# Local attention blocks: norms made per chunk, an early exponential, and ones ahead of the first block

## The chip, the cores and the metric

The kernel runs on one core of one Trainium2 chip. The metric is the device time of one execution in microseconds (us); of several runs the median is given. The engines are named as in the profile: PE is the matrix engine (PEld its weight loads), DVE the vector engine, ACT the scalar engine, POOL the GpSimd engine, and SP issues most of the transfers.

## The reference

The reference is a decoder of twelve sublayers over x of shape 16 x 64 x 128 (1024 tokens of 128 features), each followed by a residual addition and a layer norm. The change touches the third sublayer alone, a stack of two local attention layers over 16 sequences of 64 tokens. One such layer computes:

```
h = shift_token(x)                     # half of the features come from the token before
q, k, v = split(h @ wqkv)              # 8 heads of 64
q = l2norm(q) * q_scale;  k = l2norm(k) * k_scale
q, k = rotary_xpos(q, k)               # q*cos*scale + rotate_half(q)*sin*scale
o = softmax(8 * q k^T, causal in windows of 64) v
x = x + o @ wo
x = x + (a * gelu(g)) @ w2 + b2        # a, g from layernorm(shift_token(x)) @ w1 + b1
```

Here `l2norm(t)` is `t / max(norm(t), 1e-12)`. The other sublayers are attention with and without a context, a linear recurrence, and routed feed-forward layers.

## The kernel before, in words

The 1024 tokens are handled as two halves of 512. Each half is a Python generator (`first_stream`) that hands back control after every small stage, and `side_by_side` takes turns between the two halves, with half 0 five stages ahead. So the instructions of half 1's local block stand between those of half 0's local block, or of its neighbours. The program is written with a framework that schedules the instructions when it is compiled: each engine gets one fixed list, in an order that the framework chooses from what depends on what and from when buffers become free. At run time every engine goes through its list in order; an instruction that waits holds up all that stand behind it on that engine. A small change in the source can therefore change the lists around it.

The local block is `local_half(h)`. It runs two layers, and for each it works on four chunks of 128 tokens, two pairs `u` = 0 and 1 of two chunks each. The stages of a layer:

- `rotate(u)` makes, for both chunks of a pair, queries and keys on PE (L151, into a PSUM tile `qk` from a pool of two), squares them on ACT (L827), sums the squares per head on DVE (L830), multiplies by cosine tables (L834, one DVE instruction on 128 x 1024) and by sine tables with the two half-heads exchanged (L848, two DVE instructions on 128 x 512), and adds the two products on POOL (L854). The squares of both chunks are collected in one tile `ss` of 128 x 32. After the second chunk's cosine product the sums are clamped from below on DVE (L844) and rooted on ACT (L845); at the end of the stage DVE takes the reciprocal (L856). ACT holds the tables of only some functions at a time, so a root after an exponential is preceded by a table load, and so is the exponential after that.
- `values(u)` makes the values on PE and copies them from PSUM on ACT (L868).
- `flip(u)` multiplies both chunks by the reciprocals on POOL (L878), transposes them on PE (L884) and copies the result from PSUM on ACT (L885).
- `weights(u)` makes the scores on PE (L896 and a mask, L905), their maximum (L917) and the difference (L918) on DVE, and the exponential on ACT (L921). `turn(u)` transposes the weights (L930, copies L931).
- `weigh(u)` multiplies by the values (L948), divides by the sums (L958, L959 on DVE); `gather` transposes the outcome (L973, copies L974), and `put(u)` applies `wo` (L151) and adds the input (L988 on DVE).
- Then comes the feed-forward part: a shift of half the features (L151 into `psh`, copy L1020), statistics (L1026, L1028), an inverse deviation in eleven small DVE steps (L176 to L183), the normalization on DVE (L1031), six products of ones and four transposes on PE (L1040), an activation (L1044), two POOL additions for the residual (L1049, in the second layer also L1053), and the two products with the gelu between them (L1061, L1064; the PSUM tiles are `pg` and `pa`).

The ones are products of a constant matrix of ones in bf16 that `keep_busy` (L156) writes into a PSUM tile which the real work overwrites. Ahead of the first local block, cross attention (`xa`) ends with a layer norm whose output is transposed (L244) and copied to `hs` in two steps (L246, L247) between which ACT makes an exponential of the other half (L556). POOL also fills memory for a later sublayer with memsets (L417, L419) beside the last block.

Of the kernel before, what the change touches and what calls it, by code (L numbers as in the profile page):

```python
# [11 lines left out]
F32 = mybir.dt.float32  # L12
# [3 lines left out]
AF = mybir.ActivationFunctionType  # L16
ALU = mybir.AluOpType
AX = mybir.AxisListType
# [3 lines left out]
P = 128  # L22
# [15 lines left out]
class Kernel:  # L38
# [761 lines left out]
    def local_half(self, h):  # L800

        nc = self.nc
        work, psc, pt = self.aw, self.psc, self.pt
# [3 lines left out]
        for l in range(2):  # L807
            tag = f"lb{l}{h}"
# [3 lines left out]
            turned, qkT, es, eTs, oTs, aos = {}, {}, {}, {}, {}, {}  # L812

            def rotate(u):


                both = []
                ss = work.tile([P, 2, 16], F32, tag="ss", name=f"{tag}_ss{u}")
                for r in range(2):
                    c = u * 2 + r  # L820
                    qk = psc.tile([P, 2, HALF], F32, tag="sc", name=f"{tag}_qk{c}")
                    for t in range(2):
                        self.group(
                            qk[:, t, :], [(hs[:, bass.ts(c, P)], wqk[:, bass.ts(t, HALF)])]
                        )
                    t2 = self.buf(4, [2, 8, 64], f"{tag}_t2{c}")
                    nc.scalar.activation(  # L827
                        t2.rearrange("p t n d -> p (t n d)"), qk.rearrange("p t m -> p (t m)"), AF.Square
                    )
                    nc.vector.tensor_reduce(  # L830
                        ss[:, r, :], t2.rearrange("p t n d -> p (t n) d"), AX.X, ALU.add
                    )
                    t1 = self.buf(4, [2, HALF], f"{tag}_t1{c}")
                    nc.vector.tensor_tensor(  # L834
                        t1.rearrange("p t (n d) -> p t n d", d=64),
                        qk.rearrange("p t (n d) -> p t n d", d=64),
                        cos.unsqueeze(2).to_broadcast([P, 2, 8, 64]),
                        ALU.mult,
                    )
                    if r == 1:  # L840

                        root = work.tile([P, 64], F32, tag="root", name=f"{tag}_rs{u}")[:, 0:32]
                        flat = ss.rearrange("p r n -> p (r n)")
                        nc.vector.tensor_scalar(flat, flat, 1e-24, None, ALU.max)  # L844
                        nc.scalar.activation(flat, flat, AF.Sqrt)  # L845
                    for side in range(2):
                        to, of = slice(32 * side, 32 * side + 32), slice(32 - 32 * side, 64 - 32 * side)
                        nc.vector.tensor_tensor(  # L848
                            t2[:, :, :, to],
                            qk.rearrange("p t (n d) -> p t n d", d=64)[:, :, :, of],  # L850
                            sin[:, :, to].unsqueeze(2).to_broadcast([P, 2, 8, 32]),
                            ALU.mult,
                        )
                    nc.gpsimd.tensor_tensor(t1, t1, t2.rearrange("p t n d -> p t (n d)"), ALU.add)  # L854
                    both.append(t1)
                nc.vector.reciprocal(root, flat)  # L856
                turned[u] = (both, root)

            def values(u):
                for b in range(u * 4, u * 4 + 4, 2):  # L860
# [11 lines left out]
            def flip(u):  # L872

                to = self.buf(8, [8, 256], f"{tag}_qkT{u}")
                both, rs = turned.pop(u)
                for r, t1 in enumerate(both):
                    t3 = t1.rearrange("p t (n d) -> p (t n) d", d=64)
                    nc.gpsimd.tensor_tensor(  # L878
                        t3, t3, rs[:, bass.ts(r, 16)].unsqueeze(2).to_broadcast([P, 16, 64]), ALU.mult
                    )  # L880
                    for t in range(2):
                        ps = pt.tile([P, 4, P], F32, tag="t", name=f"{tag}_pf{u}{r}{t}")
                        for c in range(4):
                            nc.tensor.transpose(ps[:, c, :], t1[:, t, bass.ts(c, P)], ident)  # L884
                        nc.scalar.copy(to[:, 4 * t : 4 * t + 4, bass.ts(r, P)], ps)  # L885
                qkT[u] = to
# [92 lines left out]
            def put(u):  # L979
# [13 lines left out]
                )  # L993

            rotate(0)
            values(0)
            yield
            rotate(1)
            flip(0)
            yield  # L1000
            weights(0)
            values(1)
            yield
            turn(0)
            flip(1)
            yield
            weigh(0)
# [69 lines left out]
            if l == 0:  # L1077
                x_in = self.buf(2, [4, D], f"{tag}_x2")
                nc.vector.tensor_tensor(x_in, ps, base, ALU.add)
                self.shifted(self.psum(pt, f"{tag}_px"), h, x_in)  # L1080
                yield
            else:
                y = self.new_y("lb", h)
                nc.vector.tensor_tensor(y, ps, base, ALU.add)
                flip = self.close(pt, h, y, "lb", ones=2 + 5 * h)
                yield "last"
                flip()
# [960 lines left out]
```

## Time and profile before

| | |
|---|---|
| median of 3 runs | 878.72 us (876.24 to 880.52) |
| the profiled execution's own time | 877.26 us |
| its span, first to last instruction | 875.1 us |
| mean granted PE clock | 0.892 of full |
| PE, DVE, ACT, POOL busy | 738.4, 482.1, 354.9, 255.2 us |
| stretch of the four local blocks | from 113 to 312 us of the span |
| the add L854 | 16 times, 2354 ns |
| the scaling L878 | 16 times, 1902 ns |
| the clamp L844 | 8 times, 171 to 1490 ns |
| the reciprocal L856 | 8 times, 335 to 344 ns |
| the root L845 | 8 times, 229 to 230 ns, with 5 table loads of 1283 ns |

How to read it: a row of the chain of waits gives a start, a duration and the engine and line that the end of the program was waiting for at that time. A row of the timeline gives the start, the busy time, the engine, the line and the operation, with tiles and shapes, and in brackets how long the engine had been idle and which work released it. A row of the windows gives the stretch, its length, the busy time of PE, PEld, DVE, ACT and POOL with instruction counts, the granted clock of PE as a share of the full clock, the share of the transfer engines, and GB/s. One row can stand for several like instructions ("x2").

### The profile page before, as it was taken

Reading aid. Unit: us, or ns where it says so; the run is one execution under the profiler, and the core shown is the slowest. Engines: PE = TensorE matmul, PEld = TensorE weight load, DVE = VectorE, ACT = ScalarE, POOL = GpSimd, SP = SyncE. Lnnn points to the kernel's source line nnn. Section 1 sums busy time; section 2 is a strip of 40 time slices with the busy share of each in tenths; the row PEclk is TensorE's granted clock in tenths of the full one; section 3 lists DMA queues with packets and bytes.
Section 4 is the critical chain, followed back from the end, with each engine's and each line's share of the span. In section 5 each row is a group of like instructions: output and inputs, shape, how many; then the busy total and the mean of one; then the engine's idle time right before and its main releaser. Section 6 shows DMA issues by size and latency. Waiting matters only on the chain.

```text
span 875.1 us, 17527 instructions
## 1 busy us (share of the span) xinstructions
PE 738.4 (84%) x7115; PEld 467.3 (53%) x7117; DVE 482.1 (55%) x1103; ACT 354.9 (41%) x584; POOL 255.2 (29%) x289
## 2 busy tenths in 40 slices
PE   7888989779787899889998899958858999967991
PEld 2334547456464666457473567624534665744671
DVE  5556466674856647365446565552451856654564
ACT  1223457355454534464632454421205544511230
POOL 2324133260615412223035300035052011016632
PEclk8899989989999898999996899977967899956996
DMA  7900000000000000410000000051206632021102
GB/s 277 270 14 13 1 1 2 13 1 2 1 1 1 1 1 1 152 42 1 1 1 1 1 3 1 1 164 42 57 25 192 194 119 76 14 108 43 40 28 85
DMA packets 34504, 43.65 MB, mean 50 GB/s; under 512 B 7524, under 2 KB 26469, under 8 KB 33784
## 3 DMA queue, kind: packets, MB, share of 16 engines
q1 hardware_dynamic: 32344, 38.26, 14.1%
q0 software_dynamic: 2080, 4.26, 1.7%
q8 instruction: 58, 0.95, 0.4%
q14 instruction: 22, 0.18, 0.1%
HBM read 34.31 MB, written 11.61 MB: 52 GB/s over the span
## 4 chain that ended last, share of the span: by engine, by line
PE 52%; DVE 16%; POOL 7%; issue 6%; ACT 5%; DMA 3%; another core or an unknown queue 1%; SPq 1%; POOLq 0%; DVEq 0%; ACTq 0%
PE xa_sc L494 4%; PE xa_av L588 4%; PE xa_pt L567 3%; PE at_sc L494 2%; PE sw_pe L151 2%; PE lb_pf L884 2%; PE at_pt L567 2%; PE at_av L588 2%; POOL lb_t L878 2%; PE xa_sc L505 1%; PE lb_po L151 1%; DVE xa_e L553 1%; DVE lb_t L848 1%; PE xa_pt L156 1%; DVE lb_t L834 1%
## 5 line engine op out<-in xcount | busy, mean ns | idle before, releaser
L552 DVE TENSOR_REDUCE xa_mx<-xa_sc 128x16 f32<-128x1024 f32 x40 | 48.8, 1219 | 65.8 <-PE xa_sc L505 43.4
L854 POOL TENSOR_TENSOR lb_t<-lb_t,lb_t 128x1024 f32<-128x1024 f32 x16 | 37.7, 2354 | 98.9 <-DVE lb_t L848 94.7
L570 ACT COPY xa_eT<-xa_pt 128x512 f32<-128x512 f32 x80 | 45.0, 586 | 42.5 <-PE xa_pt L567 41.7
L156 PEld LDWEIGHTS <-ones_b 128*128 128x128 bf16 x327 | 32.2, 106 | 55.0 <-issue 36.4
L556 ACT ACTIVATE xa_e<-xa_e 128x1024 f32<-128x1024 f32 x40 | 42.3, 1058 | 44.1 <-DVE xa_e L553 44.0
L494 PE MATMUL xa_sc<-xa_km,xa_q 32*64 32x256 f32 x640 | 54.8, 407 | 1.5 <-DVE xa_e L553 0.9
L455 POOL TENSOR_SCALAR xa_km<-xa_k,const 128x512 f32<-128x512 f32 x40 | 27.3, 699 | 96.5 <-ACT xa_k L443 57.6
L567 PE MATMUL xa_pt<-const,xa_e 128*128 128x128 f32 x320 | 48.7, 279 | 2.1 <-ACT xa_e L556 2.1
L553 DVE TENSOR_TENSOR xa_e<-xa_sc,xa_mx 128x1024 f32<-128x1024 f32 x40 | 48.7, 1218 | 2.5 <-DVE xa_mx L552 0.5
L567 PEld LDWEIGHTS xa_pt<-const,xa_e 128*128 128x128 f32 x320 | 39.9, 144 | 14.6 <-ACT xa_e L556 4.6
L588 PEld LDWEIGHTS xa_av<-v,xa_eT 128*64 128x64 f32 x1280 | 40.6, 138 | 8.7 <-issue 6.5
L588 PE MATMUL xa_av<-v,xa_eT 128*64 128x18 f32 (+1 forms) x1280 | 44.4, 209 | 0.0
L151 PE MATMUL lb_qk<-w,lb_hs 128*128 128x512 f32 x64 | 34.1, 656 | 8.6 <-DVE lb_t L848 4.8
L494 PEld LDWEIGHTS xa_sc<-xa_km,xa_q 32*64 32x64 f32 x640 | 24.6, 137 | 21.6 <-issue 16.2
L830 DVE TENSOR_REDUCE lb_ss<-lb_t 128x16 f32<-128x1024 f32 x16 | 19.5, 1218 | 25.9 <-ACT lb_t L827 25.9
L205 POOL TENSOR_TENSOR rstd_xa<-mv_xa,eps 128x4 f32<-128x4 f32 x8 | 1.6, 201 | 109.7 <-DVE mv_xa L201 109.7
L156 PE MATMUL xa_pt<-ones_b 128*128 128x512 bf16 x80 | 30.3, 392 | 1.4 <-DVE xa_ao L601 1.4
L884 PE MATMUL lb_pf<-const,lb_t 128*128 128x128 f32 x128 | 22.3, 337 | 10.3 <-POOL lb_t L878 10.2
L878 POOL TENSOR_TENSOR lb_t<-lb_t,lb_rs 128x1024 f32<-128x1024 f32 x16 | 30.1, 1902 | 0.0
L151 PE MATMUL tt_ph<-tt_w,tt_xs 128*128 x40 | 23.8, 679 | 2.9 <-remote 2.9
L884 PEld LDWEIGHTS lb_pf<-const,lb_t 128*128 128x128 f32 x128 | 19.4, 177 | 12.7 <-POOL lb_t L878 11.7
L1356 POOL DMA_INDIRECT tt_got<-tt_in,tt_ids x20 | 19.6, 978 | 18.8 <-DVE tt_ids L1333 6.6
(479 smaller groups left out, 1734.0 us busy)
## 6 DMA issues: line engine op xcount, KB each, us to landing
sw_gu<-in_sw_gu SPq DMA_DIRECT2D x4, 1024.0 KB, 9.0
at_mem<-at_rsb SPq DMA_DIRECT2D x16, 256.0 KB, 2.8
at_rel<-at_mem SPq DMA_DIRECT2D x32, 128.0 KB, 3.0
w<-in_w SPq DMA_DIRECT2D x1, 3114.0 KB, 12.6
sw_dn<-in_sw_dn SPq DMA_DIRECT2D x4, 512.0 KB, 7.3
tt_w<-in_tt_w SPq DMA_DIRECT2D x2, 1024.0 KB, 8.7
tt_b<-in_tt_b SPq DMA_DIRECT2D x1, 2048.0 KB, 7.4
sw_in<-in_zeros SPq DMA_DIRECT2D x1, 1472.0 KB, 11.5
```

The source lines that it names most:

```text
L151: self.nc.tensor.matmul(out, lhsT, rhs, start=n == 0, stop=n == len(pairs) - 1)
L156: self.nc.tensor.matmul(out, self.ones_b, self.ones_b.unsqueeze(1).to_broadcast([P, 4, P]), start=True, stop=True)
L494: nc.tensor.matmul(sc[64 * j : 64 * j + 64, gg, at : at + 256], q[r, t], part[r, :, t] if local else part[r, :, :], start=not masked or (p ...
L552: nc.vector.tensor_reduce(mx, scored, AX.X, ALU.max)
L553: nc.vector.tensor_tensor(e3, scored, mx.unsqueeze(2).to_broadcast([P, 16, S]), ALU.subtract)
L556: nc.scalar.activation(e3, e3, AF.Exp, scale=scale)
L567: nc.tensor.transpose(ps[:, bass.ts(n, P)], blocks[:, bass.ts(n, P)], self.g("ident"))
L570: nc.scalar.copy(eT[:, gg, :], ps)
L588: nc.tensor.matmul(av[64 * j : 64 * j + 64, pr, hp, :, :], eT[:, gg, at : at + 64], v[:, b, hp, :, :], start=True, stop=True,)
L854: nc.gpsimd.tensor_tensor(t1, t1, t2.rearrange("p t n d -> p t (n d)"), ALU.add)
L878: nc.gpsimd.tensor_tensor(t3, t3, rs[:, bass.ts(r, 16)].unsqueeze(2).to_broadcast([P, 16, 64]), ALU.mult)
L884: nc.tensor.transpose(ps[:, c, :], t1[:, t, bass.ts(c, P)], ident)
```

## The change

The tile of sums is made per chunk (128 x 16, two buffers). Right after a chunk's sums are made they are clamped and rooted in place; the reciprocal is taken in place behind the sine products; and the scaling on POOL moves from `flip` to `rotate`, directly behind the chunk's add. At the end of the second pair a small exponential of 8 columns with scale 0 is made into a tile `ready` that nobody reads. In front of the very first product of the first block, six products of ones are written into its PSUM tile. The arithmetic of the outcome is unchanged.

```diff
-                ss = work.tile([P, 2, 16], F32, tag="ss", name=f"{tag}_ss{u}")
                 for r in range(2):
                     c = u * 2 + r
                     qk = psc.tile([P, 2, HALF], F32, tag="sc", name=f"{tag}_qk{c}")
+                    if (tag, c) == ("lb00", 0):
+                        for _ in range(6):
+                            self.keep_busy(qk[:, 0, :])
...
+                    ss = work.tile([P, 16], F32, tag="ss", name=f"{tag}_ss{c}")
                     nc.vector.tensor_reduce(
-                        ss[:, r, :], t2.rearrange("p t n d -> p (t n) d"), AX.X, ALU.add
-                    )
+                        ss, t2.rearrange("p t n d -> p (t n) d"), AX.X, ALU.add
+                    )
+                    nc.vector.tensor_scalar(ss, ss, 1e-24, None, ALU.max)
+                    nc.scalar.activation(ss, ss, AF.Sqrt)
...
-                    if r == 1:
-
-                        root = work.tile([P, 64], F32, tag="root", name=f"{tag}_rs{u}")[:, 0:32]
-                        flat = ss.rearrange("p r n -> p (r n)")
-                        nc.vector.tensor_scalar(flat, flat, 1e-24, None, ALU.max)
-                        nc.scalar.activation(flat, flat, AF.Sqrt)
...
+                    nc.vector.reciprocal(ss, ss)
                     nc.gpsimd.tensor_tensor(t1, t1, t2.rearrange("p t n d -> p t (n d)"), ALU.add)
+                    t3 = t1.rearrange("p t (n d) -> p (t n) d", d=64)
+                    nc.gpsimd.tensor_tensor(
+                        t3, t3, ss.unsqueeze(2).to_broadcast([P, 16, 64]), ALU.mult
+                    )
                     both.append(t1)
-                nc.vector.reciprocal(root, flat)
-                turned[u] = (both, root)
+                if u == 1:
+
+                    ready = work.tile([P, 8], F32, tag="ready", name=f"{tag}_ready", bufs=1)
+                    nc.scalar.activation(ready, ss[:, 0:8], AF.Exp, scale=0.0)
+                turned[u] = both
...
-                both, rs = turned.pop(u)
-                for r, t1 in enumerate(both):
-                    t3 = t1.rearrange("p t (n d) -> p (t n) d", d=64)
-                    nc.gpsimd.tensor_tensor(
-                        t3, t3, rs[:, bass.ts(r, 16)].unsqueeze(2).to_broadcast([P, 16, 64]), ALU.mult
-                    )
+                for r, t1 in enumerate(turned.pop(u)):
```

## The prediction

> **What bounds the kernel now.** I read the page's busy line and chain shares, then the chain in order of time over the local blocks, then the timeline of one block, then one-microsecond windows around the first block.
>
> ```profile
> PE 738.4 (84%) x7115; PEld 467.3 (53%) x7117; DVE 482.1 (55%) x1103; ACT 354.9 (41%) x584; POOL 255.2 (29%) x289
> ...
> PE 52%; DVE 16%; POOL 7%; issue 6%; ACT 5%; DMA 3%; another core or an unknown queue 1%; SPq 1%; POOLq 0%; DVEq 0%; ACTq 0%
> ```
>
> PE is the busiest, but only half of the chain is PE. The change touches four blocks, with their first products at 113, 163, 214 and 265 us; I call them A (layer 0, half 0), B (layer 0, half 1), C (layer 1, half 0) and D (layer 1, half 1). In the chain, C looks like this (B the same, shifted):
>
> ```profile
> 139.26 1.28 ACT L556
> ...
> 223.51 1.19 DVE lb_t L848 x2
> 224.85 0.71 POOL lb_t L854
> 225.56 1.59 issue
> 227.16 3.77 POOL lb_t L878 x2
> 230.97 0.67 PE lb_pf L884 x4
> ```
>
> Inside a block the end is set by DVE (a chunk costs 1.13 + 1.13 + 1.20 us: square sum, cosine product, two sine products), then POOL's add of the second chunk and, behind it, both scalings (3.77), then PE's flip. The first row is a table load on the path in A. The same block in the timeline:
>
> ```profile
> 221.12 2.36 POOL L854 TENSOR_TENSOR lb_t<-lb_t,lb_t 128x1024 f32<-128x1024 f32 x1 [27.92 <-DVE lb_t L848]
> ...
> 223.12 0.39 DVE L844 TENSOR_SCALAR lb_ss<-lb_ss 128x32 f32<-128x32 f32 x1
> 223.43 1.27 DVE L848 TENSOR_TENSOR lb_t<-lb_qk,lb_sin 128x512 f32<-128x512 f32 x2
> ...
> 235.48 0.17 DVE L844 TENSOR_SCALAR lb_ss<-lb_ss 128x32 f32<-128x32 f32 x1
> 235.56 1.28 DVE L848 TENSOR_TENSOR lb_t<-lb_qk,lb_sin 128x512 f32<-128x512 f32 x2
> ...
> 240.66 1.28 ACT L921 ACT_TABLE_LOAD   x1
> ...
> 241.96 1.06 ACT L921 ACTIVATE lb_e<-lb_e 128x1024 f32<-128x1024 f32 x1
> ...
> 242.94 2.20 DVE L1031 TENSOR_SCALAR lb_hn<-lb_y,lb_mv,lb_rstd 128x128 f32<-128x128 f32 x4
> 243.01 1.27 POOL L1049 TENSOR_TENSOR lb_base<-lb_y,wide 128x512 f32<-128x512 f32 x1
> ```
>
> The clamp of the norms (L844) takes 0.17 when POOL rests and 0.39 when it meets POOL's add: 223.12 + 0.39 = 223.51, the add ends at 223.48, and the next DVE instruction starts only then. So this DVE form is held until POOL's instruction ends. L1031 is held in the same way by L1049 (2.20 for four; free, they cost 0.34 each). The exponential starts 0.02 after its table load, though its input was ready at 240.83. The first block:
>
> ```profile
> 110.00:111.00 1.00, 0.62 (x3) 0.28 (x2) 1.00 (x2) 0.34 (x1) 0.00 (x0) 1.00 0.03 8
> 111.00:112.00 1.00, 0.00 (x0) 0.00 (x0) 0.37 (x1) 0.83 (x2) 0.00 (x0) 1.00 0.00 0
> 112.00:113.00 1.00, 0.00 (x0) 0.00 (x0) 0.00 (x0) 0.99 (x2) 0.00 (x0) 0.54 0.00 0
> 113.00:114.00 1.00, 0.90 (x1) 0.50 (x2) 0.00 (x0) 0.04 (x1) 0.00 (x0) 0.50 0.00 0
> ```
>
> Third figure from the right is the granted clock: it falls to 0.50 at 112.1 and returns at 118.9, just over A's first products. Their first chunk takes 3.80 us on the chain, in B 2.00.
>
> **The ones (A).** Six more 128x512 bf16 products, 0.25 each (six before the flips of L1040: 1.47). Compiled, four stand in front of the four transposes L244, the rest between them; their PSUM buffer has been free since 105.9. PE idles there (0.5 busy a microsecond), so they cost nothing to 0.15 us. PE's busy share from 108.7 to 112.1 rises from about 0.32 to 0.65; stretches of that length at 0.53 and above kept the clock (221.3 to 224.7: 0.53), one at 0.47 lost it. The first square moves from 116.91 to 115.25. If they fail, it stays.
>
> **Norms by chunk.** Per block: four clamps, roots and reciprocals of 16 columns in place of two of 32. On DVE +2 clamps (0.17 long, but the next instruction starts 0.08 later, as at 235.48) and four reciprocals for two (0.34 now for 32 columns, 0.17 for 4 columns as in L958, so about 0.24 for 16; 0.17 to the next start for 0.26): 0.32 us in all. ACT: +2 roots of at most 0.23, and the root with its table load (1.28) now stands in front of the second value copy L868, which comes 1.3 later; the weighing that reads it is a stage away, so it costs nothing, and 1.3 a block if it were not. POOL does the same 8 instructions a block, but now add, scale, add, scale: the first scaling no longer waits behind the second add. The compiled order of the changed kernel shows what this moves: the odd chunk's clamp now stands right behind its square sum, where POOL's first add is running. Behind it wait the cosine and sine products, for which PE's next product and the other half's reciprocals wait.
>
> The skill's "GPSIMD Engine Reference", section 8, names contention on the shared SBUF interfaces for two-port DVE modes, without a price. The rows give one: the hold lasts to the end of POOL's instruction. By the rule alone the clamp is a 0.17 instruction that slows somewhat (+0.1 a block); by the rows it is a stall of about 1.3.
>
> Worked for C, before to after: first sine products end 220.95 to 221.03; first add ends 223.48 to 223.55; second clamp waits 222.24 to 223.59; second sine products end 224.71 to 225.92 (+1.2). First scaling 223.63 to 225.53; second add 226.06 to 228.41, second scaling to 230.39, so the second chunk's flip starts at 230.44 instead of 230.97 (-0.5). The third square is late by 1.25 (229.0), the third sine products by 1.3 (233.7); the fourth square follows the flip's copy and is early (231.65 for 232.15); its sum waits for DVE (233.8 for 233.21), its clamp meets the last 0.1 of the third add; the fourth sine products end at 237.5 (+0.65). POOL ends the fourth scaling at 242.5 for 243.06. A new wait on POOL (the two-buffer norm tile is freed by the scaling) ends microseconds before it is asked for.
>
> **The table asked for early.** The load stands behind the last root, where ACT is free from 236.5; the 8-column exponential waits for the last reciprocal (237.6); what queues behind it is the copy L1020, due at 239. So it is hidden; without that cover it would cost its 1.28 as now, and the wait for the reciprocal besides. The exponential is then bound by its queue (value copies to 241.2): 241.2 for 241.96, -0.75. The skill's "ScalarE: Activation LUTs", What ACT_TABLE_LOAD costs, says 2.66 us with a drain per switch; here 1.28, with no gap before or after. By the page four loads would be worth 10.6 us, by the trace at most 5.1, and by the queue 0.75 a block.
>
> PE's order after that differs: all eight transposes of the weights and most flips come ahead of the four L1040, which before sat between them and waited for L1031. DVE's subtract L918 is now ahead of the statistics, so L1031 starts at 243.6 (+0.7) but no longer meets the whole of L1049: it ends at 244.6 for 245.14. Weights' transposes from 242.3, four flips at 0.85 (their pace now), hidden layer's first product at about 247.0 for 248.86: **C -1.9, B -1.9**.
>
> **D** has the memsets L417 and L419 between POOL's pieces and two POOL instructions in front of L1031:
>
> ```profile
> 294.96 3.27 DVE L1031 TENSOR_SCALAR lb_hn<-lb_y,lb_mv,lb_rstd 128x128 f32<-128x128 f32 x4
> 295.02 1.26 POOL L1049 TENSOR_TENSOR lb_base<-lb_y,wide 128x512 f32<-128x512 f32 x1
> ...
> 296.37 1.26 POOL L1053 TENSOR_TENSOR lb_base<-lb_base,xt_xa 128x512 f32<-128x512 f32 x1
> ```
>
> The same steps give 298.4 for the product at 302.5; but part is two half-clock stretches (293 to 300) that may fall elsewhere. I take -2.9 (ends -1.0 and -4.1).
>
> **A**: the square is 1.66 early, but the odd clamp costs 1.1, the extra DVE instructions 0.3, the last subtract goes behind a reciprocal of 0.35; the exponential after the load of 139.26 starts at 140.3 for 140.55. The gains of clock and table are nearly eaten: **-0.3** (-1.7 to +1).
>
> Sum -0.3 - 1.9 - 1.9 - 2.9 = -7.0. The profiled execution took 877.26 (span 875.1); so 870.3. The median of the runs shown, 878.72, lies 1.46 above it: 871.7. Later stages have the same work; their half-clock stretches may shift by one or two (1.7 each).
>
> **Rivals.** *Gain swallowed* (0.22): the +1.25 of the third square stays to the end, because PE's in-order queue carries it into the other half; only the exponential's 0.75 a block is left, -3 or less: 876.5. For it: DVE has 0.32 more to do, besides the holds; against: the fourth square is gated by the flip's copy, which is earlier.
>
> *The clamp loses the port twice* (0.14): it waits not only for the add but for the scaling behind it. Price 1.90 + 0.08 each; two in B, C and D, one in A, seven in all: +13.9 - 7.0 = +6.9, 885.6. It decides from four of the seven. For it: in D the memset started back to back with the add and the clamp took 1.49. Against: scaling depends on the add, and between dependent POOL instructions there is a gap (L1049 ends 296.29, L1053 starts 296.37) in which the first L1031 passed.
>
> *No hold at all* (0.14): in the 1.49 case the sine products behind seem to have gone on. Then 1.2 a block more is saved: 867.
>
> **Numbers.** My case (0.50) spans 868 to 877. About 0.5% (4.4 us) is what a measurement can tell from no change. Faster by more: 0.85 of my case, the no-hold case, a little of the first rival: 0.59. Within: 0.27. Slower: 0.14. Range 866 to 880.
>
> **What would show it.** Right: clock 1.00 over the first products and the first square near 115.3; odd clamps of 1.1 to 1.4 us ending with the add; scalings alternating with adds; no load in front of L921; L1040 behind the flips. Wrong: clamps of 3 us, or free ones; a half-clock stretch inside 221 to 231, where PE's share is 0.5; the distance from a block's first square to its hidden product not falling by about 2 us (32.5 now in C).

## The result, and the profile after

The changed kernel takes 869.27 us (median of 4 runs, 864.81 to 871.75), the kernel before 878.56 us beside it (4 runs, 876.24 to 880.52): ratio 0.989, 95% interval 0.9842 to 0.9937. The prediction was 871.7, within 866 to 880. Two later comparisons of the same two kernels gave 0.9901 (0.9867 to 0.9936) and 0.994 (0.9915 to 0.9965). The kernel before, compared with itself in the same way, gave 0.996 (0.993 to 0.9991), so ratios that differ by less than about half a per cent are not told apart below, and the last of these three is itself hardly clear of it.

The profiled execution took 864.81 us, its span is 863.0. The page's busy line and the chain's shares hardly move; DVE's chain share is 17% for 16%, ACT's 7% for 5%:

```profile
PE 727.1 (84%) x7121; PEld 459.1 (53%) x7123; DVE 483.9 (56%) x1119; ACT 355.3 (41%) x596; POOL 255.5 (30%) x289
...
PE 52%; DVE 17%; ACT 7%; POOL 6%; issue 5%; DMA 3%; another core or an unknown queue 1%; SPq 1%; POOLq 0%; DVEq 0%; ACTq 0%
```

What changed is inside the blocks. The chain of waits in C, in order of time:

```profile
218.98 0.16 DVE lb_ss L854
219.13 1.24 DVE lb_ss L837
220.38 1.13 DVE lb_t L840
...
222.75 1.13 PE lb_qk L151 x2
223.88 0.40 PE lb_pao L976 x2
224.28 1.71 PE lb_qk L151 x2
...
227.09 0.94 ACT lb_t L829
...
238.59 0.59 ACT lb_v L876
239.17 0.97 ACT lb_e L924
```

The clamp (L837, before L844) is now on the chain with 1.24 us, and neither the POOL add nor the scalings are: before, POOL held 4.5 us of this chain. Ahead of the exponential (L924) stands the value copy, no table load. Two pairs of like products take 1.13 and 1.71 us of the chain; the second pair ran at half clock, below. The same block in the timeline:

```profile
217.99 2.35 POOL L855 TENSOR_TENSOR lb_t<-lb_t,lb_t 128x1024 f32<-128x1024 f32 x1 [26.04 <-ACT lb_ss L838]
...
219.05 1.33 DVE L837 TENSOR_SCALAR lb_ss<-lb_ss 128x16 f32<-128x16 f32 x1
...
220.43 1.90 POOL L857 TENSOR_TENSOR lb_t<-lb_t,lb_ss 128x1024 f32<-128x1024 f32 x1
...
234.61 1.28 ACT L864 ACT_TABLE_LOAD   x1
...
239.07 1.06 ACT L924 ACTIVATE lb_e<-lb_e 128x1024 f32<-128x1024 f32 x1
```

The add ends at 220.34, the clamp at 220.38; the scaling that depends on the clamp begins 0.05 later. The four odd clamps of the first pairs took 1.33 us each and ended 0.03 to 0.04 us after their adds. The load stands 4.5 us ahead of the exponential.

Ahead of A, one-microsecond windows (third figure from the right: the granted clock):

```profile
111.00:112.00 1.00, 0.00 (x0) 0.00 (x0) 0.00 (x0) 0.98 (x2) 0.00 (x0) 1.00 0.00 0
112.00:113.00 1.00, 0.85 (x2) 0.49 (x3) 0.00 (x0) 0.09 (x1) 0.00 (x0) 1.00 0.00 0
```

The clock stays at 1.00 where it fell to 0.50 before, and A's first square is at 114.17 for 116.91. Not all of this is the ones: the last of the DVE instructions that write `y_xa`, the end of cross attention, starts at 105.34 for 106.30, and up to there all engines' lists are the same in both kernels. From it to the first square 8.83 us pass for 10.61.

Half clock comes in stretches of 3.41 us or a multiple. In C it came at another place than before. Windows of that length:

```profile
220.37:223.79 3.42, 1.36 (x4) 0.50 (x4) 3.41 (x10) 0.22 (x1) 2.85 (x2) 1.00 0.00 0
223.79:227.20 3.41, 3.41 (x12) 2.27 (x11) 0.82 (x3) 0.70 (x2) 3.30 (x2) 0.50 0.00 0
```

PE is busy 1.36 of 3.42 us while DVE works without a break (3.41), and the next stretch is granted half the clock. The products of 1.71 us in the chain fall into it.

Where the time went, from the starts of the first squares (A, B, C, D) and of D's hidden product: B's first square comes at 164.60 for 165.26, so -0.7 up to there (-1.0 up to `y_xa` and +0.3 from it); then B to C 48.57 for 51.08 (-2.5), C to D 49.81 for 51.11 (-1.3), D to its hidden product 32.20 for 35.28 (-3.1). That is -7.6 by the hidden product, and -6.6 counted from `y_xa`. The other -4.6 of the span came behind it (567.8 us for 572.4), where the lists are the same in both kernels, but for 18 small score products (0.56 us of PE) and a copy on ACT that the changed kernel has ahead of the hidden product.

### The profile page after: what moved, and what is told of

Same layout as the page of the kernel before. It is cut to its first block, busy times and chain, and to the rows that moved or that the text cites. A ratio compares the mean times of both kernels' runs of the same rounds, so it can differ in the third digit from the quotient of the medians.

```text
span 863.0 us, 17578 instructions
## 1 busy us (share of the span) xinstructions
PE 727.1 (84%) x7121; PEld 459.1 (53%) x7123; DVE 483.9 (56%) x1119; ACT 355.3 (41%) x596; POOL 255.5 (30%) x289
## 4 chain that ended last, share of the span: by engine, by line
PE 52%; DVE 17%; ACT 7%; POOL 6%; issue 5%; DMA 3%; another core or an unknown queue 1%; SPq 1%; POOLq 0%; DVEq 0%; ACTq 0%
PE xa_av L588 4%; PE xa_sc L494 4%; PE xa_pt L567 3%; PE at_sc L494 2%; DVE lb_ss L834 2%; PE sw_pe L151 2%; DVE lb_t L848 2%; DVE lb_t L840 2%; PE at_pt L567 2%; PE lb_qk L151 2%; PE at_av L588 2%; PE xa_pt L156 1%; PE xa_sc L505 1%; PE tt_ph L151 1%
## 5 line engine op out<-in xcount | busy, mean ns | idle before, releaser
L494 PE MATMUL xa_sc<-xa_km,xa_q 32*64 32x256 f32 x640 | 52.5, 393 | 2.6 <-DVE xa_e L553 2.0
L857 POOL TENSOR_TENSOR lb_t<-lb_t,lb_ss 128x1024 f32<-128x1024 f32 x16 | 30.4, 1901 | 3.1 <-DVE lb_ss L837 1.9
L887 PE MATMUL lb_pf<-const,lb_t 128*128 128x128 f32 x128 | 19.7, 295 | 8.4 <-POOL lb_t L857 7.4
L1652 POOL DMA_INDIRECT tt_out<-tt_ys,tt_outs x20 | 19.5, 975 | 18.8 <-DVE tt_ys L1651 15.2
```

The source lines that it names most:

```text
L494: nc.tensor.matmul(sc[64 * j : 64 * j + 64, gg, at : at + 256], q[r, t], part[r, :, t] if local else part[r, :, :], start=not masked or (p ...
L857: nc.gpsimd.tensor_tensor(t3, t3, ss.unsqueeze(2).to_broadcast([P, 16, 64]), ALU.mult)
```

## Experiments

All kernels ran beside the kernel before; times of different groups are compared only by their ratios, since the same kernel took 878, 861, 860 and 874 us on the chips that were used. One table first: the distances in each profile, in us. "Third square" is that of C, counted from its first square; "sum" runs from A's first square to D's hidden product. The ones move A's first square 1.8 us forward, so the sums of kernels with and without them are not alike; the column "from `y_xa`" starts at the last `y_xa` ahead of A and can be compared throughout.

| kernel | A to B | B to C | C to D | D to hidden | sum | from `y_xa` | third square |
|---|---|---|---|---|---|---|---|
| before | 48.35 | 51.08 | 51.11 | 35.28 | 185.8 | 196.4 | 11.41 |
| before, again (e5) | 48.34 | 51.09 | 51.14 | 35.12 | 185.7 | 196.3 | 11.41 |
| ones alone (e1) | 49.72 | 51.33 | 51.31 | 34.51 | 186.9 | 195.7 | 11.41 |
| early exponential alone (e2) | 47.48 | 48.72 | 48.85 | 32.15 | 177.2 | 187.8 | 11.41 |
| the same, again (e9) | 47.49 | 48.74 | 48.89 | 32.20 | 177.3 | 187.9 | 11.42 |
| norms by chunk alone (e3) | 48.53 | 49.01 | 50.36 | 33.30 | 181.2 | 191.8 | 13.93 |
| whole change | 50.44 | 48.57 | 49.81 | 32.20 | 181.0 | 189.8 | 13.82 |
| whole change, again (e6) | 51.61 | 50.18 | 49.94 | 32.22 | 183.9 | 192.8 | 13.95 |
| whole change, third (e10) | 49.98 | 48.57 | 49.93 | 32.20 | 180.7 | 189.5 | 13.94 |
| whole change without ones (e7) | 50.30 | 49.98 | 51.81 | 32.25 | 184.3 | 195.0 | 14.17 |
| clamp of two tiles (e8) | 48.99 | 50.19 | 51.41 | 32.22 | 182.8 | 191.6 | 14.04 |
| clamp as a reduction (e11) | 47.03 | 47.60 | 47.62 | 31.68 | 173.9 | 182.7 | 11.42 |
| no clamp on DVE (e4) | 46.90 | 47.34 | 47.01 | 30.63 | 171.9 | 180.7 | 11.21 |
| early exponential, no clamp (e12) | 47.74 | 48.01 | 48.02 | 32.07 | 175.8 | 186.4 | 11.11 |

### The three parts, each alone

**The ones.** The kernel before, with

```diff
+                    if (tag, c) == ("lb00", 0):
+                        for _ in range(6):
+                            self.keep_busy(qk[:, 0, :])
```

> The kernel before with the six ones alone. My theory: the ones keep the clock of the first block's first products at 1.00 (first square some 1.7 us earlier, its products 1 us instead of about 2.8), but the block's end does not follow, since a stretch of half clock opens 12 to 20 us later; time 877.5 us, 1 us under to 0.5 over the kernel before. Rival (the ones gain what they gain at the first square): 1.7 us less, 876.9 from 878.6, with the second block's first product 49.0 us after the first block's for 50.1. A second rival (the ones shift the phase of the clock for good): the unchanged stretch behind the last block's hidden product, 572.4 us before and 567.8 in the changed kernel, is near 568 and the time near 872.

Measured: ratio 0.9985 (0.9954 to 1.0016). The clock held over the first products and A's first square came 8.8 us behind `y_xa` for 10.6, but half clock came 13.2 us behind the square, and A took 49.72: at B's first square 0.4 of the 1.8 us is left. As my theory had it: no gain that can be measured. The ratio alone does not exclude the first rival's 0.998; that so little is left at A's end speaks against it. The second rival falls: its 0.992 lies outside the interval.

**The early exponential.** The kernel before, with

```diff
+                if u == 1:
+                    ready = work.tile([P, 8], F32, tag="ready", name=f"{tag}_ready", bufs=1)
+                    nc.scalar.activation(ready, root[:, 0:8], AF.Exp, scale=0.0)
```

> The kernel before with the early exponential of eight columns alone, which reads the shared root of the second half. My theory: the score exponentials lose the table load of 1.28 us behind the masks, in the second, third and fourth blocks, but the load before the hidden activation stays behind them; 0.75 us a block, so 876 us from 878.6. Rival (each load taken off the path is worth all of its 1.28 us, in all four blocks): 5.1 us, 873.5. A third view (the path through the flips decides the exponential's start anyway, so nothing): 878.6.

Measured: ratio 0.9858 (0.981 to 0.9906), and in a second run (below) 0.9855. All three views expected too little: 0.997 by my theory, 0.994 by the boldest. B and C are 2.3 us shorter, D 3.1, A 0.9. Part of the reason shows in windows of 3.41 us ahead of the hidden product of C. The kernel before, in its second profile (e5), and then the early exponential alone, in its second profile (e9):

```profile
241.65:245.06 3.41, 1.52 (x11) 1.12 (x12) 2.98 (x9) 1.46 (x2) 2.30 (x2) 1.00 0.00 0
245.06:248.48 3.42, 3.42 (x18) 3.42 (x17) 0.00 (x0) 2.84 (x6) 0.00 (x0) 0.50 0.00 0
```

```profile
235.20:238.60 3.40, 2.77 (x19) 1.79 (x18) 2.99 (x18) 2.33 (x4) 3.40 (x3) 1.00 0.00 0
238.60:242.00 3.40, 3.24 (x37) 2.36 (x35) 1.42 (x4) 3.20 (x6) 0.56 (x1) 1.00 0.00 0
```

In the kernel before PE is busy 1.52 of 3.41 us, loses the clock, and makes the flips ahead of the hidden product at half clock. With the early exponential it is busy 2.77 of 3.40 and keeps it. C's exponential comes 24.65 us after the first square for 25.62, and the hidden product 5.9 us after the exponential for 7.0.

The first of these windows begins where the table load (240.32 to 241.60) has ended. PE waits in it twice, for the exponential that the load made late and then for the normalization (L1031), which POOL holds (2.21 us for its four instructions, 1.15 in e3):

```profile
242.72 0.55 PE L930 MATMUL lb_pt<-const,lb_e 128*128 128x128 f32 x3 [1.66 <-ACT lb_e L921]
...
244.08 0.33 PE L1040 MATMUL lb_phn<-const,lb_hn 128*128 128x128 f32 x1 [0.82 <-DVE lb_hn L1031]
```

With the early exponential the first wait is 0.24 us and the second is gone, since the flips now stand ahead of L1040. The load alone did not cost the clock: norms by chunk alone (below, e3) keep the clock at this place. In B they have the same wait of 1.66 us for the exponential, but none for the normalization, and PE's share is 0.51:

```profile
191.64 0.55 PE L926 MATMUL lb_pt<-const,lb_e 128*128 128x128 f32 x3 [1.66 <-ACT lb_e L917]
```

```profile
189.83:193.25 3.42, 1.76 (x15) 1.47 (x15) 2.52 (x13) 2.50 (x4) 1.98 (x2) 1.00 0.00 0
193.25:196.66 3.41, 3.41 (x21) 2.37 (x19) 0.00 (x0) 3.39 (x7) 0.00 (x0) 1.00 0.00 0
```

In the kernel before, with the second wait as well, it is 0.45. How much of the gain belongs to the missing load and how much to the new order of the lists, which came with it, no run separates.

**Norms by chunk.** The changed kernel less the ones and less the early exponential:

```diff
-                    if (tag, c) == ("lb00", 0):
-                        for _ in range(6):
-                            self.keep_busy(qk[:, 0, :])
...
-                if u == 1:
-
-                    ready = work.tile([P, 8], F32, tag="ready", name=f"{tag}_ready", bufs=1)
-                    nc.scalar.activation(ready, ss[:, 0:8], AF.Exp, scale=0.0)
```

> The changed kernel without the ones and without the early exponential: the norms by chunk alone. My theory: most of the gain is here, about 4 us, 874.5 us; the second, third and fourth block from first square to the next first square or the hidden product 1 to 2.5 us shorter, the odd chunks' clamps 1.3 us. Rival (the unchanged stretch behind the last block's hidden product, 572.4 before and 567.8 after, is what shortened, and it hangs on the ones or the exponential): blocks shorter all the same, but that stretch back at 572, and 873 at the lowest. A rival that gives the gain to the table load: 877.

Measured: ratio 0.9942 (0.9914 to 0.997), B, C and D 2.1, 0.8 and 2.0 us shorter. The size is what I expected (0.9954), but it is not most of the gain: the early exponential alone gives more than twice as much. Behind D's hidden product it had 549.8 us, with 90 us of half clock there; the nearest profile of the kernel before, on another chip (e5), had 555.7 and 112.

### The clamp

**No clamp on DVE.** The changed kernel, with the root made of the sum plus 1e-24 (the clamp is left out, so a sum is changed by 1e-24):

```diff
-                    nc.vector.tensor_scalar(ss, ss, 1e-24, None, ALU.max)
-                    nc.scalar.activation(ss, ss, AF.Sqrt)
+                    nc.scalar.activation(ss, ss, AF.Sqrt, bias=self.tiny)
```

> The changed kernel with the clamp taken from VectorE: the root is made of the sum plus 1e-24 instead of the greater of sum and 1e-24 (a difference of 1e-24 in the sum), so there is no operation left that is held while GpSimd adds. My theory: the hold of the odd clamp (1.33 us for 0.17) goes, second sine products start 1.2 us earlier, and since they set the third and fourth scaling, a block gains about 1 us: 865.5 us from 869.3. Rival (the hold only fills time in which the second add would wait for GpSimd anyway, the first add and scaling taking 4.3 us): 869, same. Second rival (another operation of VectorE is held in the clamp's place, the sum or the reciprocal): 869 to 870, with that row at 1.3 us.

Measured: ratio 0.9805 (0.9751 to 0.9859), the shortest blocks of all, and better than the 0.985 expected. But here other things move too: the framework puts the fourth product of a block ahead of a flip and the roots elsewhere in ACT's list. So it shows that a better version exists, not what the hold costs.

**The clamp of two tiles.** This one and the next leave every list as it is and change only the form of the clamp.

```diff
-                    nc.vector.tensor_scalar(ss, ss, 1e-24, None, ALU.max)
+                    nc.vector.tensor_tensor(ss, ss, self.tiny, ALU.max)
```

> The changed kernel with the clamp written as the greater of two tiles (a tile of 1e-24 made once by GpSimd) in place of the tile and a constant; every engine's list is otherwise the same. My theory: the hold belongs to the form, as the reciprocal, which runs in the middle of GpSimd's add (0.24 us), and the products are not held; the odd clamps take 0.2 us for 1.33, the blocks get 1 to 2 us shorter each, ratio near 0.978, as without a clamp (0.9805). Rival (any instruction that reads two tiles of SBUF is held; the products read one operand from PSUM): the odd clamps take 1.3 us as before and the time is the changed kernel's. Second rival (the hold is off, but the blocks' ends follow GpSimd's four adds and scalings): clamps 0.2 us and the time the changed kernel's, within 0.2%.

Measured: ratio 0.9911 (0.9882 to 0.994), the changed kernel's own beside it 0.9901. The first rival was right. C's odd clamp and the add, in the timeline:

```profile
219.97 2.35 POOL L857 TENSOR_TENSOR lb_t<-lb_t,lb_t 128x1024 f32<-128x1024 f32 x1 [26.06 <-ACT lb_ss L840]
...
220.86 0.24 DVE L856 RECIPROCAL lb_ss<-lb_ss 128x16 f32<-128x16 f32 x1
221.02 1.33 DVE L839 TENSOR_TENSOR lb_ss<-lb_ss,tiny 128x16 f32<-128x16 f32 x1
```

The reciprocal passes in the middle of POOL's add in 0.24 us; the clamp of two SBUF tiles behind it is held for 1.33, to the add's end.

**The clamp as a reduction.** The reduction over the squares had never been held, so the clamp was written as one:

```diff
                     nc.vector.tensor_reduce(
-                        ss, t2.rearrange("p t n d -> p (t n) d"), AX.X, ALU.add
+                        pair[:, :, 0], t2.rearrange("p t n d -> p (t n) d"), AX.X, ALU.add
                     )
-                    nc.vector.tensor_scalar(ss, ss, 1e-24, None, ALU.max)
+                    nc.vector.tensor_reduce(ss, pair, AX.X, ALU.max)
```

> The changed kernel with the clamp written as a reduction: the sums are written into every second column of a tile of 128 x 16 x 2 whose other columns hold 1e-24, and the greater of each pair is taken by a reduction; every engine's list is otherwise the same. The sums of squares, also reductions, ran in 1.21 us beside GpSimd's adds. My theory: the reduction is not held, the odd clamps take 0.15 to 0.25 us for 1.33, the third square comes 1.2 us earlier, 2.4 where the half clock goes too; ratio 0.976 to 0.983. Rival (held all the same, as the two-tile form was): 1.33 us, ratio 0.989. Second rival (the hold is off, but GpSimd's adds and scalings set the end): clamps 0.2 us and ratio 0.988 to 0.991.

Measured: ratio 0.9806 (0.9751 to 0.986), the changed kernel's beside it 0.994 (0.9915 to 0.9965); medians 861.18 and 869.98 us. In C:

```profile
215.70 2.37 POOL L859 TENSOR_TENSOR lb_t<-lb_t,lb_t 128x1024 f32<-128x1024 f32 x1 [26.32 <-ACT lb_ss L842]
...
216.76 0.14 DVE L841 TENSOR_REDUCE lb_ss<-pair 128x16 f32<-128x32 f32 x1
```

```profile
219.05:222.46 3.41, 3.18 (x16) 2.00 (x16) 2.08 (x10) 0.66 (x2) 3.33 (x3) 1.00 0.00 0
```

The clamp takes 0.14 us under the add (1.33 before), and in the stretch ahead of the third square PE is busy 3.18 us instead of 1.36. That stretch lies 1 us later in the block than the other; from 7.2 to 10.6 us behind the first square, as in the changed kernel, PE is busy 2.53 of 3.41. C's third square comes 11.42 us after the first, for 13.94. My theory held, the middle of its range. A hold of 1.2 us costs 1.0 in a block where the clock stays (B, 48.57 to 47.60) and 2.3 where it does not (C, 49.93 to 47.62). Some luck is in it: right behind the third square, in B as in C, PE's share falls to 0.47 for a whole stretch of 3.41 us, and the clock stayed, as it does in only about half of such cases (last section).

### The parts together

**The kernel before, again** (no edit).

> The kernel before once more, so that it has a profile on the same chip as the runs beside it. My theory: the half-clock stretch in front of the flips of the second, third and fourth block (194.0, 245.2 and 296.4 us in the first profile) is no accident: TensorE idles while the exponential waits for its table, a block is 51.1 us long and so 15 of the gate's stretches of 3.41 us, and it stays in step; the new profile shows half clock between the exponential and the hidden product in at least two of the three blocks, which last 51.0 to 51.4. Rival (it fell there by chance in one execution): none or one of the three. Ratio 1.000.

Its profile has half clock 29.0 to 29.1 us after the first squares of B, C and D, as the first profile had (28.7 to 29.0): three of three, no accident.

**The changed kernel, again** (no edit), second and third profile.

> The changed kernel once more, beside the parts of it. My theory (the early exponential is the larger part, the norms by chunk give part of their gain back to the held clamp): ratio 0.982 to 0.989, near that of the early exponential alone (0.986), the blocks from the second on 48.5 to 50. Rival (the parts add up: 0.986 times 0.994): 0.980. In the first block the half clock at 128 to 132 comes again, behind the wait for the scaling that the held clamp delays; if it does not, the first block is 1.5 us shorter than in the first profile (50.4).

> The changed kernel a third time. My theory: ratio 0.988 to 0.991, as twice before; half clock within 16 us of the first square in at least two of the four blocks, and the distance from first square to exponential 25.9 to 28 us in the third block, for 24.65 with the early exponential alone. Rival (the half clock there was chance): in one block or none, the distance 25.9, and the time that of the early exponential alone.

Ratios 0.9901 and 0.994. Both lie outside what was expected of them (0.982 to 0.989, then 0.988 to 0.991), on the slow side, and the parts do not add up to 0.980. In the third profile C's exponential comes 26.02 us after the first square, as expected. Half clock came 9.4 to 10.6 us after the first square, before the third, in A, B and C of the second profile, in A and C of the third, in C of the first (there in A 14 us after it). A without any half clock was not seen in the changed kernel.

**Without the ones.** The changed kernel, with

```diff
-                    if (tag, c) == ("lb00", 0):
-                        for _ in range(6):
-                            self.keep_busy(qk[:, 0, :])
```

> The changed kernel without the six ones. My theory: the ones are worth nothing at the end of the first block, ratio within 0.3% of the changed kernel's. Rival (they keep the clock and are worth the 1.7 us of the first square): 0.2% slower than the changed kernel, with the second block's first square 1.5 us or more later. A third view (they harm, by moving the half clock to 128): faster by 0.2%, the first block 48.5 us long.

Measured: ratio 0.9918 (0.9887 to 0.995) for 0.9901 beside it. A's first square at 115.89 for 113.95, B's at 166.19 for 165.56: of 1.9 us 0.6 are left at A's end (0.1 of both lies ahead of `y_xa`). In the times that is not told apart from nothing.

**The early exponential alone, beside the whole change.**

> The kernel before with the early exponential alone, once more, beside the whole change on one chip. My theory (the early exponential is the gain; norms by chunk, set on top of it, cost, as the held clamp lengthens TensorE's idle time before the third square and with it the half clock): ratio 0.981 to 0.986, at least 0.4% under the whole change's. Rival (the two were measured on different chips, and the whole change is as fast): equal within 0.3%.

Measured: ratio 0.9855 (0.9812 to 0.9897), median 862.42, for the whole change 0.994 and 869.98. The intervals do not meet: one part of the change is faster than all of it, by 7.6 us. Only some of that is seen in the blocks: from `y_xa` to D's hidden product the early exponential takes 187.9 us, the whole change 189.5 to 192.8. In these two profiles 7.4 us lie behind the blocks (568.5 for 575.9), where the lists are the same. Why is open.

**The early exponential and no clamp, norms by pairs.** As e2, and the clamp is left out as in e4:

```diff
-                        nc.vector.tensor_scalar(flat, flat, 1e-24, None, ALU.max)
-                        nc.scalar.activation(flat, flat, AF.Sqrt)
+                        nc.scalar.activation(flat, flat, AF.Sqrt, bias=self.tiny)
```

> The early exponential alone, with the norms still by pairs of chunks and the clamp taken from VectorE (the root is made of the sum plus 1e-24). It asks whether norms by chunk are needed at all for the 0.9805 of the changed kernel without a clamp. My theory: norms by chunk without a hold are worth some 1 us a block, so this one stays behind: 0.983 to 0.986, as the early exponential with its clamp (0.17 and 0.39 us). Rival (all of that gain comes from the missing clamps and what else the lists put in another order): 0.980 or under.

Measured: ratio 0.9821 (0.9765 to 0.9878), between the two theories. The blocks B and C are 48.0 us, the reduction's 47.6: freed of the hold, norms by chunk are worth about 0.4 us a block more than norms by pairs. The three fastest kernels (e4 0.9805, e11 0.9806, e12 0.9821) are not told apart, and none of them from the early exponential alone: beside each other e11 took 861.18 us and e9 862.42, though e11 is 5.2 us shorter from `y_xa` to the hidden product. What shortens the blocks does not all arrive in the time. Beside the changed kernel e11 is faster; e4 was not run beside it.

## Why the prediction was right, and where it was not

The time was right, and so was its sum up to D's hidden product (-7.0 predicted, -7.6 found, -6.6 of it from `y_xa` on). The path in each block was mostly right too, but not what each part of the change is worth. That the sum came out is in part luck: A +0.3 for -0.3, B -2.5 and C -1.3 for -1.9 each, D -3.1 for -2.9. The median fell by 9.3 us; the rest lies where the lists are nearly the same. Step by step:

- **The ones (A).** The clock held, and the ones are worth 1.8 us at the first square where 1.66 was worked out: from `y_xa` to it 10.6 us pass in each profile without them, 8.8 in each with them. That the square came at 114.17 for 115.25 is the 1.0 us by which that profile was ahead already. That A's end would keep almost nothing (-0.3) holds within its bounds (+0.3 from `y_xa`), but the reason was short of one term: half clock that comes back 10 to 14 us later in all three profiles of the changed kernel. With the clamp of two tiles (e8), which is held as long, it did not come back in A, and 1.1 us were left at A's end. In the first profile the flip of the second chunk waited 2.05 us for POOL, and the fourth chunk's products behind it took 3.12 us at half clock.
- **The odd clamp.** "Its clamp waits to the end of POOL's instruction", about 1.3: found 1.33 in all four. (In the prediction's own row the next DVE instruction starts at 223.43, 0.05 before the add's end, and not only then, as it says.) The rivals *loses the port twice* and *no hold at all* fall: the dependent scaling starts 0.08 us behind the add's end, and the clamp passes there.
- **The third square late by 1.25.** In B it is late by 1.20 (12.58 for 11.38), in C by 2.41 (13.82 for 11.41). The prediction had named a half-clock stretch inside 221 to 231 as a sign of being wrong, and it came in C, at 223.8: PE's share ahead of it, 0.5 then, fell to 0.40 because of the hold. It added 1.2 us to the hold's own 1.2.
- **POOL's four scalings.** The second ends 14.00 us after C's first square for 14.58, -0.6 where -0.5 was expected. The fourth ends 27.36 after it for 26.72, while -0.56 was expected: the same half clock.
- **The exponential and the hidden product.** Expected 24.9 us after the first square; found 24.66 in B and 25.90 in C. From there to the hidden product 5.8 was expected, 5.56 found. B gave -2.4 to its hidden product, C -1.2, for -1.9 each; D -3.1 for -2.9. (D's half clock ahead of its hidden product was at 296.4 to 303.2 before, not 293 to 300 as the prediction has it; after, there is none in its place.)
- **The table asked for early, -0.75.** This is the term that was mis-sized. Alone it gives 2.1 to 2.6 us in B and C from first square to hidden product. Two things were missing. The wait that the load causes and the wait for L1031 together cost PE its clock ahead of the flips, three blocks of three. And the new order of lists (flips ahead of L1040, L918 ahead of the statistics), credited to the change as a whole, belongs to this exponential: with it alone the lists move in the same way. So *gain swallowed*, with "only the exponential's 0.75 a block" left, was priced far too low.
- **Norms by chunk as a gain.** They are one alone (0.9942), where they too end the half clock ahead of B's and C's hidden product. On top of the early exponential nothing of that is left to gain, and the hold remains: from `y_xa` to the hidden product it is 189.5 to 192.8 with them and 187.9 without. The gains of the two parts do not add; both remove the half clock ahead of the hidden product.
- **Behind D's hidden product**, -4.6 in the first pair of profiles was not foreseen, and it does not come with the change each time: in the third profile of the changed kernel that stretch took 575.9 us, more than the 572.4 before. Half clock is a part of it (120 us of it there in the first profile after, 139 before, 136 in the third), the rest is open.

Which forms are held is what the Trainium skill, "SBUF — State Buffer", section "SBUF: two separate sides", says: a GpSimd instruction and a VectorE instruction in a two-port mode (or one with two SBUF inputs, if the GpSimd instruction reads SBUF) exclude each other; the one that starts first has the shared ports for its whole length. The runs agree in each form tried: the two-tile clamp is held (1.33 us), the one-source reduction and the reciprocal are not (0.14, 0.24). That the clamp against a constant runs in a two-port mode is read from its hold; no run shows the mode by itself. The prediction had used the page on GpSimd alone, whose sentence gives no length, and took the length from a row, rightly.

Open stays what the ones are worth in time, and how the early exponential's gain divides between the load and the order.

## What to carry to other kernels

Take a change apart before keeping it: here one of three parts alone was faster than all three together. Where PE's share in a stretch of 3.4 us is near one half, price each wait once for itself and once for the clock: here a wait of 1.2 us cost 2.3. Compare from a point ahead of the first edit: 1.0 us of the gain in the first pair of profiles lay ahead of it. A small DVE instruction that is moved beside a long POOL instruction costs what is left of the latter, if its form is one that is held; a one-source reduction in its place was free.

## What the hardware showed that was not expected

- Between 160 and 300 us of all fourteen profiles, full-clock stretches of 3.41 us were followed by half clock in all 28 cases with a PE share of 0.40 or less, and in 9 of 17 from 0.41 to 0.51; of some 490 above that, two lost it (0.513 and 0.557). No idle stretch as long as 3.41 us is needed: the Trainium skill, "TensorE: Matmul & The Clock Gate", section "HAM oscillation — how this bites in real kernels", warns of idle gaps above some 3.4 us, while here a share of 0.40 over one such stretch was enough.
- A block of 51.1 us is 15 such stretches (51.2), so in the kernel before the half clock came at the same place of block after block; blocks of 48 to 50 us drift against it.
- The same kernel before took 878 us in one group of runs and 860 in another (874 on chip 1, 860 on chip 9), with equal blocks (185.8 and 185.7 us in the profiles). Of the 16.7 us that the span is shorter behind D's hidden product, 5.1 come some 300 us and 8.3 some 495 us behind it, in the routed layers.
